# A fused attention and gated-FFN layer on one core: the ending of a sequence spread over three steps, and its TensorE pieces issued ahead of the value matmuls

## The chip, the core and the metric

The kernel runs on one core of a Trainium2 chip. A core has a matrix engine (TensorE, "PE" in the profile; its weight loads are "PEld"), a vector engine (VectorE, "DVE"), an engine for activations (ScalarE, "ACT"), a general engine (GpSimd, "POOL"), and a queue from which the transfers of this kernel are issued (SyncE, "SP"). Each engine takes its instructions in the order in which they were written, and waits at the head of its queue. The metric is the device time of one execution in microseconds (us).

## What is computed

The input x has 8 batches of 2048 tokens of 512 channels in fp32. Cut to what matters:

```python
xn = layernorm(x)
q, k = xn @ Wq.T + bq, xn @ Wk.T + bk          # 8 heads of 8 channels
v = xn @ Wv.T + bv                             # 8 heads of 64 channels
scores = leaky(q . k / sqrt(8), 0.2)           # per head, 2048 x 2048
s = gamma * (softmax(scores) @ v) + xn
ret = softmax(gate logits of xn), all but the largest of 4 set to 0
g = silu(xn @ W.T + sum_e ret[e] * (xn @ Wd[e].T) @ Wu[e].T)
out = x + s * g
```

## The kernel before, in words

**Sequences and steps.** A sequence `s` is one pair of heads on one block of 512 queries, so a batch has 4 pairs x 4 blocks = 16 sequences and the program 128. A sequence has 16 steps `i`, one for each 128 keys; the program has 2048 steps, all written out by one Python loop, with no scheduler behind it: `tc.manual_schedule()` keeps the written order on every engine. "Half step" in the change's title is one such step. In each step the loop issues, in this order:

- PE: subtract the row maximum from the scores of this step, first head (`less_max`, L658); scores of the next step (`score`, L641, two matmuls); one unit of row maxima of the next sequence (`max_unit`, L586, two matmuls, which VectorE reduces at L597 in 1.2 us); `less_max` for the second head.
- ACT: two exponentials of 512 columns (L670), then two leaky ReLUs of the next scores (L652).
- then one call of `half_full` (batches 0 to 6) or of `half_light` (the last batch, which has no next batch to project). It fills the rest of the step on PE: values, or pieces of other work.
- POOL: the exponentials are added up for the softmax's denominator (`add_up`, L702), in 15 of a sequence's 16 steps.

A **value** (`weigh`, L682) multiplies one step's exponentials with v; it runs some steps late, from the list `last`. One value is two matmuls, which the trace shows as four records.

**Pieces.** Three generators are advanced piece by piece: `queue[0]` is the *ending* of the sequence that has had its last value, `queue[1]` is `shift_rows` (row maxima made into a shift for the next sequence; L603 to L630), and `queue[2]` is the background work: `project_block` (q, k and v of the next batch) and `lift_block` (the gated FFN). What a generator yields is its state: IDLE (go on at any time), TINY or FREE or SLOW (a piece with a PSUM bank comes next), HOLD (in the middle of an accumulation), WAIT (vector work follows in the next step). A generator in HOLD or WAIT keeps the others out. `go_on` advances whoever is IDLE, and then one that is in WAIT, and says so by its result. `spent` and `due` keep the background work in step with a plan.

**One bank.** In the loop there is one PSUM bank for pieces, tag "m" (`ps_m`, one buffer). The ending's two tiles (`dps2`, `atp`) and every tile of the background work (`zps`, `pps`, `dps`, `nps`, `gps`, `rps`, `vps`, `tp`) go through it, so a piece's first matmul waits until the piece before has been read out for the last time. The row maxima have a bank of their own pair of banks (`mx`), one buffer too: the matmuls of one step wait for the L597 of the step before.

**The ending** (`ending`, L719 to L762). VectorE copies the sums of values out (L724); some idle turns later come two TINY pieces and a WAIT:

1. L737: four groups of small matmuls (8 records) sum the denominators over partitions; VectorE multiplies by a mask, adds up, and takes the reciprocal (L745, L747, L749).
2. L754: four transposes; VectorE multiplies by the reciprocal (L756) and adds xn (L757).
3. In the next step, after WAIT: VectorE multiplies by the gate (L760) and adds x (L761), and SP issues the store. L761 is the last reader of the bank.

In steps 1 and 2 `half_full` issues one value, then the piece (L861 to L864). In step 3 `go_on` returns true and `half_full` issues up to two values and nothing else. `half_light` goes on after `go_on` instead: in the same step it issues the next background piece, and one or two values.

`lift_block` yields WAIT as well: after the gate's softmax (L461), its pick (L472), and twice around the split of the expert outputs (L498, L504).

Of the kernel before, what the change touches and what calls it, by code (L numbers as in the profile page):

```python
# [12 lines left out]
ALU = mybir.AluOpType  # L13
# [19 lines left out]
def fused_layer_kernel(  # L33
# [37 lines left out]
    nc = tc.nc  # L71
# [3 lines left out]
    CH = NB * NT  # L75
# [168 lines left out]
    TINY, SLOW, WAIT, HOLD, FREE, IDLE = 5, 4, 3, 2, 1, 0  # L244
# [4 lines left out]
    def spend(cost):  # L249
        spent[0] += cost  # L250
# [273 lines left out]
    def where(s):  # L524
        return s // SEQ, s % NPAIR, (s % SEQ) // NPAIR
# [150 lines left out]
    def weigh(s, i, ex):  # L676

        if i == 0:
            avt[s] = ps_av.tile([128, BLK], FP, name="av")
        v_sb = vts[s]  # L680
        for e in range(2):
            nc.tensor.matmul(  # L682
                avt[s][64 * e : 64 * e + DV, :],
                lhsT=v_sb[:, i, 64 * e : 64 * e + DV],
                rhs=ex[:, e, :],
                start=(i == 0),
                stop=(i == CH - 1),
            )
        if i == CH - 1 and s + 1 < B * SEQ:
            assert queue[0] is None  # L690
            queue[0] = ending(s)
            state[0] = next(queue[0])
# [13 lines left out]
    def read_for_ending(s):  # L706

        b, p, n = where(s)
        if s >= B * SEQ or s in reads or (b, n) not in lifted:
            return  # L710
        cols = slice(p * 128, (p + 1) * 128)
        gs = two.tile([128, NT, 128], FP, name="gs")
        nc.sync.dma_start(out=gs, in_=GS[b][n][:, :, cols])
        xs = two.tile([128, 2, NT, 128], FP, name="xs")
        nc.sync.dma_start(out=xs[:, 0], in_=xv[b, n][:, :, cols])
        nc.sync.dma_start(out=xs[:, 1], in_=XN[b][n][:, :, cols])
        reads[s] = gs, xs

    def ending(s):  # L719

        b, p, n = where(s)
        cols = slice(p * 128, (p + 1) * 128)
        avs = two.tile([128, BLK], FP, name="avs")
        nc.vector.tensor_copy(avs, avt.pop(s))  # L724
        yield IDLE
        sums = acc.pop(s)
        while s not in reads:
            read_for_ending(s)
            yield IDLE
        gs, xs = reads.pop(s)  # L730
        for _ in range(3):
            yield IDLE
        yield TINY

        dps = ps_m.tile([128, 2, NT, 32], FP, name="dps2", tag="m")
        for q in range(4):
            nc.tensor.matmul(  # L737
                dps[32 * q : 32 * q + 32],
                lhsT=ones[:, 0:32],
                rhs=sums.rearrange("p e (t q j) -> p e t q j", t=NT, q=4)[:, :, :, q, :],  # L740
                start=True,
                stop=True,
            )
        dv = dps.rearrange("p e t j -> p (e t) j")
        nc.vector.tensor_tensor(dv, dv, diag.unsqueeze(1).to_broadcast([128, 2 * NT, 32]), ALU.mult)  # L745
        rd = sm.tile([128, NT, 2, 1], FP, name="rd")
        nc.vector.reduce_sum(rd.rearrange("p t e o -> p e t o"), dps, axis=AX.X)  # L747
        rd = rd.rearrange("p t e o -> p (t e) o")
        nc.vector.reciprocal(rd, rd)  # L749
        spend(0.5)  # L750
        yield TINY
        tp = ps_m.tile([128, NT, 128], FP, name="atp", tag="m")
        for t in range(NT):
            nc.tensor.transpose(tp[:, t, :], avs[:, t * 128 : (t + 1) * 128], ident)  # L754
        tv = tp.rearrange("p t (e d) -> p (t e) d", e=2)
        nc.vector.tensor_tensor(tv, tv, rd.to_broadcast([128, NT * 2, DV]), ALU.mult)  # L756
        nc.vector.tensor_tensor(tp, tp, xs[:, 1], ALU.add)  # L757
        spend(0.5)
        yield WAIT
        nc.vector.tensor_tensor(tp, tp, gs, ALU.mult)  # L760
        nc.vector.tensor_tensor(gs, tp, xs[:, 0], ALU.add)  # L761
        nc.sync.dma_start(out=ov[b, n][:, :, cols], in_=gs)  # L762

# [49 lines left out]
    def go(j):  # L813
        state[j] = next(queue[j], None)
        if state[j] is None:
            queue[j], state[j] = None, IDLE
        holder[:] = [k for k in range(3) if state[k] in (HOLD, WAIT)]

    def ahead():

        return holder or [k for k in (1, 0, 2) if queue[k] is not None and state[k] != IDLE]

    def go_on():

        for j in range(3):
            if queue[j] is not None and state[j] == IDLE:
                go(j)
        if holder and state[holder[0]] == WAIT:
            go(holder[0])
            return True  # L830
        return False
# [6 lines left out]
    last = []  # L838
    ended = [False]

    def values(count):
        for w in last[:count]:
            weigh(*w)
        del last[:count]

    def half_full():


        run = 0
        for w in last[:2]:  # L850
            run += 1
            if w[1] == CH - 1:
                break
        alone = run and last[0][1] == CH - 1
        if go_on():
            values(run)
            return
        j = (ahead() or [None])[0]
        if j == 2 and state[2] != HOLD and spent[0] > due[0] + AHEAD:
            j = None  # L860
        if j is not None and state[j] == TINY:  # L861
            values(min(run, 1))
            go(j)
            ended[0] = True  # L864
        elif j is None or len(last) > MUCH - (state[j] != HOLD) or (ended[0] and run > 1):
            ended[0] = False
            for g in stats.values():
                next(g, None)
            values(run)
        else:  # L870
            if alone:
                values(1)
            go(j)
            if state[j] == HOLD and not alone:
                go(j)
            ended[0] = state[j] != HOLD

    def half_light():

        begun = spent[0]  # L880
        go_on()
        late = last and (state[2] == SLOW or last[0][1] == CH - 1)
        if late:
            values(1)
        j = (ahead() or [None])[0]
        while j is not None and state[j] != WAIT and spent[0] < begun + 0.8 and (j < 2 or spent[0] < due[0]):
            go(j)
            if state[j] != HOLD:
                break
        if not late:  # L890
            values(2 if spent[0] - begun < 0.4 and len(last) > 1 and last[0][1] < CH - 1 else 1)
# [7 lines left out]
    with tc.manual_schedule():  # L899
# [143 lines left out]
        for s in range(B * SEQ):  # L1043
            for i in range(CH):
                if i <= 3 and s + 2 not in qst and (where(s + 2)[0] in (0, *ready) or i == 3):
                    load_stacks(s + 2)
                if i >= 6 and s + 1 not in vts and (where(s + 1)[0] in valued or i == 13):
                    load_values(s + 1)
                if i >= 12:
                    read_for_ending(s)  # L1050
                due[0] = due_at(s + (i + 1) / CH)
                u = s * CH + i + CH + LEAD
                nxt = s * CH + i + 1


                less_max(s, i, sc0, 0)
                if nxt < total:
                    sc1 = score(nxt // CH, nxt % CH)
                max_unit(u // CH, u % CH, flip=True)
                less_max(s, i, sc0, 1)  # L1060
                if u % CH == CH - 1 and u < total:
                    queue[1], state[1] = shift_rows(u // CH), IDLE
                ex = exp(sc0)
                if nxt < total:
                    leaky(sc1)
                if s < (B - 1) * SEQ:
                    half_full()
                else:
                    half_light()
                add_up(s, i, ex)  # L1070
                last.append((s, i, ex))
                sc0 = sc1
        values(len(last))
        for _ in ending(B * SEQ - 1):
            pass
# [44 lines left out]
```

## Time and profile before

| what | us |
|---|---|
| median of three runs (5580.12 to 5607.04) | 5593.03 |
| the profiled execution, its own time | 5602.28 |
| its span in the trace | 5600.5 |
| up to the first step of the loop | 139.5 |
| batches 0 to 6: 1792 steps | 4744.8 |
| last batch: 255 steps, up to the start of the last | 699.9 |
| the last step and the last ending | 16.3 |
| PE busy, POOL busy, ACT busy, DVE busy | 5408.1, 4778.7, 4440.4, 3678.3 |
| mean granted clock of PE | 0.961 |

The four stretches come from cutting the timeline at the first L658 matmul of each step. A row of a timeline reads: start, duration, engine, line, operation, tile written <- tiles read, shapes, count, and in brackets how long the engine had been idle before and whose end it was waiting for. A step is named below by what PE does in it after its fixed part, in records of the trace's lines: "one value", "two values", "two matmuls" of a projection.

### The profile page before, as it was taken

What the parts mean: (1) busy time and instruction counts of PE and PEld (TensorE: products, weight loads), DVE (VectorE), ACT (ScalarE), POOL (GpSimd) and SP (SyncE); (2) the same over time, 40 slices, a digit from 0 to 9 for tenths busy, and PEclk for the clock granted to TensorE, in tenths of its full rate; (3) what the DMA queues carried; (4) which work ended last, traced back from release to release, by engine and by line L of the source; (5) the groups of instructions that cost most, each with busy time, mean ns of one, the idle gap of its engine ahead of it and who ended that gap; (6) DMA issues with size and microseconds to landing.
All of it is one profiled execution on the core that took longest, in us unless ns stands there. A gap on an engine that the chain in (4) does not pass through costs nothing.

```text
span 5600.5 us, 78233 instructions
## 1 busy us (share of the span) xinstructions
PE 5408.1 (97%) x26258; PEld 2008.9 (36%) x26258; DVE 3678.3 (66%) x4990; ACT 4440.4 (79%) x8627; POOL 4778.7 (85%) x2906
## 2 busy tenths in 40 slices
PE   7999999999999999999999999999999999989998
PEld 3333333333333333333333333333333333333332
DVE  5577666667677666666666766676666766655653
ACT  1788888878888788887878878888788888867777
POOL 1789988888989888888988889898889898878878
PEclk9999999999999999998989989999999999989988
DMA  5333433434324343252422434225333333322221
GB/s 190 114 115 118 134 108 95 119 103 153 103 80 145 87 152 95 79 156 78 155 86 89 139 101 143 85 89 156 100 126 97 108 118 119 108 78 78 71 63 61
DMA packets 528265, 615.39 MB, mean 110 GB/s; under 512 B 44092, under 2 KB 438332, under 8 KB 491768
## 3 DMA queue, kind: packets, MB, share of 16 engines
q1 hardware_dynamic: 527864, 610.39, 35.3%
q8 instruction: 209, 3.42, 0.3%
q14 instruction: 192, 1.57, 0.1%
HBM read 407.88 MB, written 202.38 MB: 109 GB/s over the span
## 4 chain that ended last, share of the span: by engine, by line
PE 82%; ACT 7%; DVE 6%; issue 2%; DMA 1%; POOL 1%; SPq 0%; POOLq 0%; ACTq 0%; DVEq 0%
PE av L682 30%; PE sc L658 17%; PE zps L279 9%; PE vps L279 8%; PE mx L586 7%; ACT ex L670 4%; PE pps L265 2%; PE qkps L265 2%; PE dps L265 2%; ACT sc L652 2%; DVE mxr L597 2%; PE dps L737 1%; POOL acc L702 1%; PE atp L754 1%; PE gps L446 1%
## 5 line engine op out<-in xcount | busy, mean ns | idle before, releaser
L702 POOL TENSOR_TENSOR acc<-acc,ex 128x1024 f32<-128x1024 f32 x1792 | 4230.5, 2361 | 301.3 <-ACT ex L670 187.2
L597 DVE TENSOR_REDUCE mxr<-mx 128x2 f32<-128x1024 f32 x2030 | 2477.3, 1220 | 1249.9 <-PE sc L658 1017.6
L670 ACT ACTIVATE ex<-sc 128x512 f32<-128x512 f32 x4096 | 2229.2, 597 | 949.3 <-PE sc L658 772.0
L652 ACT ACTIVATE sc<-sc 128x512 f32<-128x512 f32 x4096 | 2238.0, 593 | 19.6 <-PE sc L641 19.6
L682 PE MATMUL av<-ex,v_sb 128*64 128x512 f32 x8192 | 2156.8, 632 | 11.6 <-DVE avs L724 9.2
L658 PE MATMUL sc<-shift,ones_r 2*128 2x512 f32 x4096 | 1683.7, 466 | 62.5 <-ACT sc L652 48.5
L586 PE MATMUL mx<-k,q_sb 32*128 32x512 f32 x4096 | 1460.6, 457 | 17.3 <-DVE mxr L597 11.9
L658 PEld LDWEIGHTS sc<-shift,ones_r 2*128 2x128 f32 x4096 | 706.2, 188 | 1555.7 <-ACT sc L652 1455.0
L641 PE MATMUL sc<-q_sb,k 32*128 32x512 f32 x4096 | 1046.7, 507 | 0.0
L682 PEld LDWEIGHTS av<-ex,v_sb 128*64 128x64 f32 x8192 | 469.8, 138 | 842.4 <-issue 807.9
L279 PE MATMUL zps<-w_sb,xnT 128*128 128x512 f32 (+1 forms) x1120 | 559.4, 614 | 23.8 <-DVE gs L761 10.5
L586 PEld LDWEIGHTS mx<-k,q_sb 32*128 32x128 f32 x4096 | 568.3, 189 | 38.8 <-DVE mxr L597 20.4
L702 POOL TENSOR_TENSOR acc<-ex 128x1024 f32<-128x1024 f32 x128 | 301.9, 2358 | 211.3 <-ACT ex L670 211.3
L279 PE MATMUL vps<-wv_sb,xnT 128*128 128x512 f32 x960 | 473.4, 617 | 7.4 <-DVE gs L761 7.2
L641 PEld LDWEIGHTS sc<-q_sb,k 32*128 32x128 f32 x4096 | 388.9, 187 | 0.8 <-issue 0.8
L279 PEld LDWEIGHTS zps<-w_sb,xnT 128*128 128x128 f32 x1120 | 192.2, 196 | 271.2 <-issue 250.6
L279 PEld LDWEIGHTS vps<-wv_sb,xnT 128*128 128x128 f32 x960 | 163.5, 189 | 207.7 <-issue 193.9
L518 DVE SCALAR_TENSOR_TENSOR g<-th,zps 128x512 f32<-128x512 f32 x128 | 88.0, 688 | 194.8 <-ACT th L517 194.8
L611 POOL TENSOR_TENSOR ml<-m,big 128x8 f32<-128x8 f32 x128 | 26.2, 205 | 133.5 <-DVE m L610 133.5
L265 PE MATMUL dps<-xnT,wd_sb 128*128 128x512 f32 (+1 forms) x280 | 138.6, 604 | 0.7 <-DVE gs L761 0.7
L349 DVE TENSOR_TENSOR vb<-vps,bv_sb 128x512 f32<-128x512 f32 x120 | 82.9, 691 | 85.5 <-PE vps L279 82.5
L265 PE MATMUL pps<-xnT,wp_sb 128*128 128x512 f32 (+1 forms) x280 | 130.9, 585 | 3.5 <-DVE gs L761 3.5
(124 smaller groups left out, 2675.8 us busy)
## 6 DMA issues: line engine op xcount, KB each, us to landing
v_sb<-VS SPq DMA_DIRECT2D x127, 1024.0 KB
k<-KS SPq DMA_DIRECT2D x256, 256.0 KB
XN<-xn SPq DMA_DIRECT2D x32, 1024.0 KB
q_sb<-QS SPq DMA_DIRECT2D x256, 128.0 KB
xnT<-XT SPq DMA_DIRECT2D x32, 1024.0 KB
GS<-g SPq DMA_DIRECT2D x32, 1024.0 KB
gs<-GS SPq DMA_DIRECT2D x128, 256.0 KB
xs<-in_x_dram SPq DMA_DIRECT2D x128, 256.0 KB
```

The lines of the kernel that those rows point to most:

```text
L265: nc.tensor.matmul(ps[:, part], lhsT=wt[:, c, :], rhs=xnT[c][:, part], start=(c == 0 and part.start == 0), stop=(c == NC - 1 and part.stop ...
L279: nc.tensor.matmul(ps[:, part], lhsT=xnT[c][:, t * 128 : (t + 1) * 128], rhs=wt[:, c, part], start=(c == 0 and part.start == 0), stop=(c = ...
L349: nc.vector.tensor_tensor(vb[:, :, t, :], ps.rearrange("p (h d) -> p h d", h=NPAIR), bv_sb.rearrange("p (h d) -> p h d", h=NPAIR), ALU.add,)
L518: nc.vector.scalar_tensor_tensor(g[:, t, :], th, 1.0, ps, ALU.add, ALU.mult)
L586: nc.tensor.matmul(parts[e], lhsT=q_sb[r, t * 128 : (t + 1) * 128], rhs=k_sb[r, kb // 2 * BLK : (kb // 2 + 1) * BLK], start=True, stop=True,)
L597: nc.vector.reduce_max(mxr[s][:, :, t, kb : kb + 1], mx, axis=AX.X)
L641: nc.tensor.matmul(sc[e], lhsT=k_sb[r, i // 2 * 128 : (i // 2 + 1) * 128], rhs=q_sb[r, :], start=True, stop=True,)
L652: nc.scalar.activation(sc[e], sc[e], AF.Prelu, alpha=SLOPE)
L658: nc.tensor.matmul(sc[e], lhsT=ones_r[r, :], rhs=shifts[s][r, :], start=False, stop=True, skip_group_check=True,)
L670: nc.scalar.activation(ex[:, e, :], sc[e], AF.Exp, scale=qscale)
L682: nc.tensor.matmul(avt[s][64 * e : 64 * e + DV, :], lhsT=v_sb[:, i, 64 * e : 64 * e + DV], rhs=ex[:, e, :], start=(i == 0), stop=(i == CH ...
L702: nc.gpsimd.tensor_tensor(acc[s], old, ex, ALU.add)
```

## The change

The ending's vector work is spread over one step more: the addition of xn moves from the transposes' step to the next, and the addition of x, with the store, from there to a third, behind a second WAIT. In `half_full` the ending's two TINY pieces are issued ahead of the value of their step (pieces of the background work still go behind it). In `half_light` a step in which `go_on` has resumed a generator from WAIT, of the ending or of the background work, issues values alone, two if two wait and the first isn't a sequence's last, else one, and returns.

```diff
@@ ending
         nc.vector.tensor_tensor(tv, tv, rd.to_broadcast([128, NT * 2, DV]), ALU.mult)
-        nc.vector.tensor_tensor(tp, tp, xs[:, 1], ALU.add)
         spend(0.5)
         yield WAIT
+        nc.vector.tensor_tensor(tp, tp, xs[:, 1], ALU.add)
         nc.vector.tensor_tensor(tp, tp, gs, ALU.mult)
+        yield WAIT
         nc.vector.tensor_tensor(gs, tp, xs[:, 0], ALU.add)
         nc.sync.dma_start(out=ov[b, n][:, :, cols], in_=gs)
@@ half_full
         if j is not None and state[j] == TINY:
+
+            if j == 0:
+                go(j)
             values(min(run, 1))
-            go(j)
+            if j != 0:
+                go(j)
             ended[0] = True
@@ half_light
         begun = spent[0]
-        go_on()
+        if go_on():
+            values(2 if len(last) > 1 and last[0][1] < CH - 1 else 1)
+            return
         late = last and (state[2] == SLOW or last[0][1] == CH - 1)
```

The built programs' order of instructions differs as follows. In batches 0 to 6, 111 endings of each kernel have both pieces in this loop; the counts of steps by content are nearly the same before and after (two values 618 and 616, one value alone 105 and 119, ending pieces 222 and 222), but the order of them around endings and gates isn't. In the last batch the steps with one value alone go from 66 to 81, and those with two or three matmuls of `zps` beside a value from 18 to 35.

## The prediction

> **What bounds the kernel.** I read the page first: its shares, and the slices of the granted clock.
>
> ```profile
> span 5600.5 us, 78233 instructions
> ...
> PE 5408.1 (97%) x26258; PEld 2008.9 (36%) x26258; DVE 3678.3 (66%) x4990; ACT 4440.4 (79%) x8627; POOL 4778.7 (85%) x2906
> ...
> PEclk9999999999999999998989989999999999989988
> ```
>
> PE is the bound on the whole, and its clock dips in some slices. Next I cut the timeline of all 2048 steps at their first L658. Undisturbed steps come out alike: two values 2.53 us, two projection matmuls 2.57, an ending piece with one value 2.24 to 2.47, one value alone 2.22 (ACT sets that one). Taking such a row for each step of batches 0 to 6 gives 4444 us; they took 4745. The 300 between are the question. By place: 117 in 80 steps at half clock; at full clock 73 in the ending's three steps and the one behind (5, 22, 3 and 43); 110 elsewhere, most of it in runs of transposes, which the change leaves alone. The step behind the ending takes 3.10 us in the mean.
>
> Who waits for the ending's last vector instruction:
>
> ```profile
> L761 DVE TENSOR_TENSOR gs<-atp,xs x128: 690/691/693, 221.4 to 5596.1; 128x512 f32<-128x512 f32 x128
> ...
>   PEld gps L446: 13.0, 16
>   PEld vps L279: 12.5, 12
>   PE zps L279: 10.5, 9
> ...
>   PE nps L425: 8.2, 3
> ```
>
> Every one is a piece that needs the one bank. Then the worst case, in the timeline:
>
> ```profile
> 2564.43 2.16 DVE L609 TENSOR_SCALAR big<-m 128x8 f32<-128x8 f32 x1
> 2567.43 0.70 DVE L757 TENSOR_TENSOR atp<-atp,xs 128x512 f32<-128x512 f32 x1
> 2568.04 1.22 DVE L597 TENSOR_REDUCE mxr<-mx 128x2 f32<-128x1024 f32 x1
> 2569.31 0.76 PE L586 MATMUL mx<-k,q_sb 32*128 32x512 f32 x2 [1.70 <-DVE mxr L597]
> 2569.89 0.69 DVE L761 TENSOR_TENSOR gs<-atp,xs 128x512 f32<-128x512 f32 x1
> 2572.33 1.87 PE L446 MATMUL gps<-simn,pw 128*128 128x4 f32 x8
> ```
>
> A small instruction (L609) takes 2.16 us, its median being 0.16: it began inside a POOL addition (L702) and ended with it. VectorE is then too late for the step's maxima, and PE stands idle 1.70 us. What the clock does is in the stretches of this place (span, then PE, PEld, DVE, ACT, POOL busy, then granted clock):
>
> ```profile
> 2562.00:2565.50 3.50, 3.50 (x26) 1.70 (x24) 3.18 (x6) 2.89 (x7) 3.42 (x2) 1.00 0.00 0
> 2565.50:2569.40 3.90, 2.20 (x13) 0.57 (x9) 3.83 (x6) 2.32 (x5) 3.19 (x8) 1.00 0.00 0
> 2569.40:2600.00 30.60, 30.60 (x90) 10.85 (x90) 15.49 (x30) 16.58 (x33) 22.52 (x10) 0.50 0.22 62
> ```
>
> After 3.9 us with PE busy for 2.2, the clock is 0.50 for 30.6 us. Light steps stay under it: one value alone takes 3.06 instead of 2.22. The clock changes only at multiples of 3.41 us, and every such stretch with PE busy below 0.56 of it is followed by half clock, most of those above 0.8 are not.
>
> **The Trainium skill on this.** TensorE: Matmul & The Clock Gate (section "Why this matters for your kernels") asks for no PE-idle gap above some 3 us, one window of idleness being what halves the clock. By that a gap of 1.70 us could not have done it, the half clock would come from elsewhere and stay, and the sum below would be 5507. The row above contradicts it, so I go by the row.
>
> **Part 1, the ending over three steps.** Vector work per step before: L597 1.22 plus 0.43, 0.42, 0.20; 1.22 plus 0.70, 0.70; 1.22 plus 0.69, 0.69. The last two are 2.6 us each in steps of 2.47 and 2.53, so L761 ends 1.46 us into the fourth step, where a piece could start at 0.66. After: 1.92, 2.61, 1.91. The third sheds what the second left over: from a third step whose maxima are ready at 0.76, addition and L760 end 0.85 into the next, its L597 ends at 2.08 and the last addition at 2.77, which is 0.24 into the fifth. A piece there starts at 0.66 and finds the bank free. So the 43 us go, and the second and third steps' 3. SP's store moves by one step with its instruction; what stands behind it in that queue is the shift's small loads for a sequence that begins several steps later, cost nothing; if that cover were gone, one step, 2.5 us, an ending. The fourth step holds values alone: two in 82 of 111 endings, one in 29. That costs only if later steps get heavier; by the built order all counts together move the undisturbed sum by 0.7 us.
>
> **What follows from it, the half clock.** Of the 28 gates (`gps`) in batches 0 to 6, six stand directly behind an ending with the long L609 in its second step; their twelve steps take 35.2 to 43.4 us against 30.24 of an undisturbed row. A seventh (38.6) and four with three one-value steps around them lose another 22. In the built order after, no gate stands there: 13 follow the fourth step in the undisturbed row's own sequence, 8 stand behind matmuls as in rows that kept the clock, 7 have two steps of two values behind them. L609 stands three steps ahead of the ending in those six sequences. I keep four half-clock stretches of 3.3 us (as at the slow `nps` of step 819): 15 of 117.
>
> **Part 2, the ending's pieces ahead of the value.** Undisturbed, nothing is won: in the last batch, where both orders occur, the two steps sum to 4.73 us either way (2.48 and 2.25, or 2.25 and 2.48). What is lost is cover: the first piece needs the bank, whose reader may not be done. After the last `zps` of a block L518 ends 1.43 into the step; after `pps`, L421 at 1.58; after `dps`, L442 at 0.69. How long PE stands is shown in the last batch, where the piece went first already:
>
> ```profile
> 5136.82 0.75 DVE L421 TENSOR_SCALAR pw<-pps,bp_sb 128x512 f32<-128x512 f32 x1 [1.17 <-ACT pw L420]
> ...
> 5137.71 0.64 PE L737 MATMUL dps<-acc,ones 128*32 128x256 f32 x8 [0.98 <-POOL acc L702]
> ```
>
> PE starts about 0.11 behind L421; the additions it reads were done over 7 us before, so POOL, though named, isn't it. By the built order 21 endings follow such a `zps`, 7 a `pps`, 13 a `dps`: 21 x (1.54 - 0.66) + 7 x 1.03 + 13 x 0.14 = 27 us, 22 above what the first step lost. Where it stalls, ACT catches up and the second step is 0.2 shorter: 28 x 0.2 = 6 back. In 36 endings L609 and L610 (0.40 together) now stand ahead of the first piece's vector work, 0.15 each at the transposes: 5; in 14 of them POOL may still be behind from a norm (L310, 1.02), from 0 to 1.2 us each; I take 0.5, from the long L609s two steps behind a norm: 7. Of the other bound, a gain, nothing: the reciprocal comes earlier, but its reader waits for L597.
>
> **Part 3, the last batch.** Its 255 steps took 699.9 us. There `half_light` starts the next piece in the very step in which vector work is resumed, and PE meets its own wait: 17 steps of 4.77 to 7.40 us (gates, norms, splits, the first `zps` behind an ending), 62 over the 2.45 of their neighbours, and 18 steps at half clock behind them (ten of 3.06, eight of 4.21), 23 more. With values alone in such steps the wait lies under them. Given back: 17 more steps with a second or third `zps` matmul at 2.65 for 2.39, less 15 of one value at 2.22, so 2; new half-clock steps 5. That leaves 622. POOL then decides: 240 additions of 2.43 (five in 12.14) and 16 chains of six (1.7) and three norms give 614, just below.
>
> **Sum.** 139.5 ahead + batches 0 to 6: 4445 (undisturbed) + 110 + 27 + 16 (second step, 22 - 6) + 12 + 15 = 4625, + 622 + 16.3 = 5403; with the 1.8 between span and time, 5405, against 5602.3 of the profiled execution. That one lay 9 above the median; I leave it there, since the clock's luck is in both.
>
> **Rivals.**
> - *The half clock stays* (0.15). The stalls go, but light steps or the new stalls of Part 2 fall into as many of the 3.41 us stretches: 5405 + 102 = 5507. For it: the 28 new stalls of 0.9 to 1.0 leave PE busy for about 0.72 to 0.76 of a stretch, and such were followed by half clock about one time in six. Against it: dense steps follow, which at once restore the clock (3.3 us at step 819, not 13).
> - *POOL is the bound of the last batch* (0.10). Its chains wait for VectorE 1.05 us each (133.5 in 127 times), its norms 1.0: 614 + 17 + 3 = 634, so 5417. For it: 614 of 622. Against it: seven buffers of exponentials lie between.
> - *Slower: gates starve* (0.04). The fourth step eats the store of values, so gates run over one-value steps and every gate falls to half clock, as six did, at 11 us each: 28 x 11 = 308 instead of 15, giving 5698. It decides from about 19 gates on (197 / 11 = 18 beyond those kept); with 16 to 20 of them the time is within half a per cent, another 0.03. Against it: the built order has a step of two values behind every gate.
> - *The change doesn't do what it says* (0.06): a third step that VectorE enters late, so that the wait only moves to the fifth step. Then the 43 stay, and the half clock by half: 5405 + 43 + 51 = 5499.
>
> **Chances.** The forecast has 0.62. The range runs from 5350 (no half clock 15, no price for L609 12, the last batch at POOL's 614, and 20 of the 110 gone) to 5510, which takes in the first, second and fourth rival's times. Faster are the forecast and those three. Half a per cent, 28 us, is about what a measurement of this kernel can tell from no change. Faster 0.93, same 0.03, slower 0.04.
>
> **What would show it.** L761's successor no longer in the list of waits; the step behind the ending at 2.5; first pieces behind `zps` starting 1.5 into their step; PE's granted clock near 0.98; no step above 4.5 in the last batch. Wrong it is if the clock stays at 0.96, or if steps with one value follow gates in rows.

## The result, and the profile after

The change makes the kernel slower, by three quarters of a per cent. The median of six runs is 5635.03 us (5619.47 to 5662.39), against 5598.75 of six runs of the kernel before: a ratio of 1.0076, 95% interval 1.005 to 1.0101. The forecast was 5405, and its range ended at 5510. The profiled execution of the changed kernel took 5627.17, its span is 5625.2, and the mean granted clock rose only from 0.961 to 0.966.

The page of the kernel after: its span, the engines' busy time, the granted clock by slice.

```profile
span 5625.2 us, 78283 instructions
...
PE 5346.8 (95%) x26258; PEld 1977.6 (35%) x26258; DVE 3672.9 (65%) x4990; ACT 4447.3 (79%) x8627; POOL 4779.3 (85%) x2906
...
PEclk9999999999999999989999899999999999999999
```

PE does the same 26258 matmuls in 61 us less busy time, in a span that is 25 longer. So PE is idle 86 us more than before, and the time is to be looked for in waits. First, who waited for the ending's last vector instruction, now L762 (kernel after, instructions of that line):

```profile
L762 DVE TENSOR_TENSOR gs<-atp,xs x128: 647/680/691, 219.2 to 5620.8; 128x512 f32<-128x512 f32 x128
...
  PEld nps L425: 0.7, 3
  PEld gps L446: 0.7, 3
```

The long list that stood under L761 is gone, and the step behind the ending takes 2.47 us in the mean instead of 3.10. What the change was built to do, it does. Now rows from PE's list of waits in the kernel after (engine, its tile and line, whose end it waited for: us in all, times, longest):

```profile
PE mx L586 <- DMA q_sb<-QS: 63.2, 17, 7.3
PE tp L370 <- ACT xn L319: 47.0, 28, 1.7
PE dps L737 <- DVE g L518: 17.5, 21, 0.8
...
PE dps L737 <- DVE pw L421: 7.9, 8, 1.0
```

and the same pairs in the kernel before:

```profile
PE mx L586 <- DMA q_sb<-QS: 2.0, 2, 1.2
PE tp L370 <- ACT xn L319: 1.7, 1, 1.7
```

The lower two of the first list are the price that Part 2 had foreseen, each within 1 us: 21 waits of 0.83 and 8 of 1.0. The upper two are new, 106 us together, and nothing in the prediction names them. No line of the diff touches either.

**The norm.** One of the 28 waits at L370, all engines of the kernel after (start, duration, engine, line, and in brackets the idle time before and its end):

```profile
1145.68 1.08 PE L682 MATMUL av<-ex,v_sb 128*64 128x512 f32 x4
...
1147.55 1.53 ACT L319 ACTIVATE xn<-xt,nmr,rstd 128x512 f32<-128x512 f32 x2
...
1148.43 0.66 PE L370 MATMUL tp<-ident,xn 128*128 128x128 f32 x4 [1.67 <-ACT xn L319]
```

The first transposes of a projected block read what ACT's L319 has normalized. L319 is written at the end of a generator (`norm`), and `half_full` advances those generators only in its branch for values alone (`for g in stats.values(): next(g, None)`), not in a step that has resumed somebody from WAIT. One more WAIT an ending turns 111 steps of the first kind into steps of the second, while the work goes on at the same pace. The norm is then not finished when its block begins, `project_block` runs what is left of it on the spot, and L319 stands in the same step as the transposes that read it: in the built order so in all 28 blocks of batches 0 to 6, where before it stood 1 to 11 steps ahead in nearly all. What the wait costs is more than itself (kernel after, stretches: span, then PE, PEld, DVE, ACT, POOL busy, granted clock, DMA share, GB/s):

```profile
1143.00:1146.40 3.40, 3.40 (x16) 1.19 (x14) 2.51 (x3) 2.87 (x6) 3.24 (x2) 1.00 0.00 0
1146.40:1149.80 3.40, 1.73 (x14) 0.84 (x14) 1.27 (x3) 2.88 (x6) 2.34 (x1) 1.00 0.83 307
1149.80:1153.20 3.40, 3.40 (x14) 1.30 (x14) 1.89 (x3) 2.58 (x5) 2.35 (x1) 0.53 0.01 4
```

PE is busy for 1.73 of 3.40, and the next stretch runs at 0.53 of the clock.

**The loads of q.** The SP queue of the kernel after (SPq is an issue, its duration the time that the queue was held by it):

```profile
1090.89 1.30 SPq L338 DMA_DIRECT2D KS<-hi  x2
1092.30 1.20 SPq L338 DMA_DIRECT2D KS<-lo  x2
1093.54 0.57 SPq L343 DMA_DIRECT2D QS<-hi  x1
...
1095.38 0.84 SPq L343 DMA_DIRECT2D QS<-lo  x1
1096.27 0.52 SPq L389 DMA_DIRECT2D XN<-xn  x1
1096.83 0.70 SPq L390 DMA_DIRECT2D XT<-xnT  x1
1097.64 2.84 SPq L542 DMA_DIRECT2D k<-KS  x2
1100.53 2.98 SPq L548 DMA_DIRECT2D q_sb<-QS  x2
```

and PE beside it, a little later:

```profile
1103.31 0.50 PE L641 MATMUL sc<-q_sb,k 32*128 32x512 f32 x2
1110.69 0.79 PE L586 MATMUL mx<-k,q_sb 32*128 32x512 f32 x2 [6.89 <-DMA q_sb<-QS]
```

A block's split issues ten stores, the last two (XN and XT) of 1 MB each. Behind them stand the four loads of k and q that a later sequence needs. They are written at step 0 of a sequence, and the first row maxima that read them at step 5. Since the background work has moved against the sequences, the split's stores now start at step 0 or 14 in three of four blocks of a batch (0, 14, 14 and 7), and in those three nothing stands between them and the loads; before they started at steps 12, 6, 6 and 2 (in the first batch 14, 7, 7 and 3). The loads are issued 7 us late, their own issue takes 2.8 to 3.0 us for two where 1.3 is usual, and q lands 7 us behind it. All the long waits stand at step 5 of a sequence; in sequence 6 of every batch that step takes 10.8 to 11.9 us.

Cut into steps as for the prediction, with what it had forecast for each term, and with kernel e6, which is told below (us). The 12 us that the prediction put at the transposes are counted in the second step, where these stand. The undisturbed row is worked out from the counts of steps alone, so it can't show what went wrong.

| term | before | forecast | after | e6 |
|---|---|---|---|---|
| up to the loop | 139.5 | 139.5 | 138.1 | 138.1 |
| batches 0 to 6, undisturbed | 4444.2 | 4445 | 4444.9 | 4444.9 |
| half clock (steps) | 117.1 (80) | 15 | 198.9 (100) | 22.4 (12) |
| ending's first step | 4.9 | 27 | 47.4 | 35.9 |
| second, third step | 25.7 | 28 | 26.4 | 26.8 |
| step behind | 42.7 | 0 | 0.4 | 1.2 |
| elsewhere | 110.2 | 110 | 115.6 | 111.4 |
| last batch | 699.9 | 622 | 635.4 | 644.3 |
| last step and last ending | 16.3 | 16.3 | 18.0 | 16.1 |

The row of the half clock holds most of the wait for q (54 of 63 us), since the steps with the long waits end under it, and 10 of the norm's 47. The norm's other 37 stand in the row "elsewhere", which 39 of the 112 steps of transposes have left for the half clock. The row of the half clock is 184 above the forecast, and the whole is 222 above it. The time that the clock itself spent at one half rose less than the row: by the trace's clock records it was 262.4 us of batches 0 to 6 before and 308.7 after, 33.0 of these while PE waited for q. In e6 it is 42.5.

### The profile page after: what moved, and what is told of

The parts are those of the page before. It is cut to its first block, busy times and chain, and to the rows that moved or that the text cites. A ratio compares the mean times of both kernels' runs of the same rounds, so it can differ in the third digit from the quotient of the medians.

```text
span 5625.2 us, 78283 instructions
## 1 busy us (share of the span) xinstructions
PE 5346.8 (95%) x26258; PEld 1977.6 (35%) x26258; DVE 3672.9 (65%) x4990; ACT 4447.3 (79%) x8627; POOL 4779.3 (85%) x2906
## 4 chain that ended last, share of the span: by engine, by line
PE 83%; ACT 8%; DVE 3%; DMA 3%; issue 1%; SPq 1%; POOL 1%; ACTq 0%; POOLq 0%; DVEq 0%
PE av L682 30%; PE sc L658 17%; PE zps L279 9%; PE vps L279 8%; PE mx L586 7%; ACT ex L670 5%; ACT sc L652 3%; PE qkps L265 2%; PE pps L265 2%; DMA q_sb<-QS 2%; PE dps L265 2%; PE atp L754 1%; PE dps L737 1%; PE tp L370 1%; DVE mxr L597 1%
## 5 line engine op out<-in xcount | busy, mean ns | idle before, releaser
L702 POOL TENSOR_TENSOR acc<-acc,ex 128x1024 f32<-128x1024 f32 x1792 | 4231.5, 2361 | 270.8 <-ACT ex L670 154.9
L597 DVE TENSOR_REDUCE mxr<-mx 128x2 f32<-128x1024 f32 x2030 | 2484.3, 1224 | 1311.6 <-PE sc L658 1021.3
L658 PE MATMUL sc<-shift,ones_r 2*128 2x512 f32 x4096 | 1652.8, 463 | 77.8 <-ACT sc L652 67.1
L586 PE MATMUL mx<-k,q_sb 32*128 32x512 f32 x4096 | 1475.1, 453 | 67.1 <-DMA q_sb<-QS 63.2
L658 PEld LDWEIGHTS sc<-shift,ones_r 2*128 2x128 f32 x4096 | 694.2, 187 | 1668.9 <-ACT sc L652 1562.0
L586 PEld LDWEIGHTS mx<-k,q_sb 32*128 32x128 f32 x4096 | 579.7, 188 | 84.7 <-issue 71.2
L279 PE MATMUL zps<-w_sb,xnT 128*128 128x512 f32 (+1 forms) x1120 | 529.0, 589 | 7.9 <-DMA xnT<-XT 7.9
L702 POOL TENSOR_TENSOR acc<-ex 128x1024 f32<-128x1024 f32 x128 | 301.8, 2358 | 183.4 <-ACT ex L670 183.3
L518 DVE SCALAR_TENSOR_TENSOR g<-th,zps 128x512 f32<-128x512 f32 x128 | 88.0, 688 | 184.8 <-ACT th L517 184.8
L611 POOL TENSOR_TENSOR ml<-m,big 128x8 f32<-128x8 f32 x128 | 26.2, 205 | 208.9 <-DVE m L610 202.0
L373 DVE COPY xnT<-tp 128x512 f32<-128x512 f32 x112 | 77.3, 690 | 106.1 <-PE tp L370 105.7
```

Source lines behind the costliest of these rows:

```text
L279: nc.tensor.matmul(ps[:, part], lhsT=xnT[c][:, t * 128 : (t + 1) * 128], rhs=wt[:, c, part], start=(c == 0 and part.start == 0), stop=(c = ...
L518: nc.vector.scalar_tensor_tensor(g[:, t, :], th, 1.0, ps, ALU.add, ALU.mult)
L586: nc.tensor.matmul(parts[e], lhsT=q_sb[r, t * 128 : (t + 1) * 128], rhs=k_sb[r, kb // 2 * BLK : (kb // 2 + 1) * BLK], start=True, stop=True,)
L597: nc.vector.reduce_max(mxr[s][:, :, t, kb : kb + 1], mx, axis=AX.X)
L658: nc.tensor.matmul(sc[e], lhsT=ones_r[r, :], rhs=shifts[s][r, :], start=False, stop=True, skip_group_check=True,)
L702: nc.gpsimd.tensor_tensor(acc[s], old, ex, ALU.add)
```

## The experiments

Two theories stood against each other. *The order*: Part 1's extra step moves the background work against the sequences; the norm starves and the loads fall behind the stores, and both drag the clock down. *The pieces*: Part 2's stalls at the first pieces bring the half clock, as the first rival had it. Each ratio is against the kernel before on the same chip. The kernels are called e1 to e10.

**One part at a time.** The last batch's edit alone, on the kernel before (e1):

```diff
@@ half_light (kernel before)
-        go_on()
+        if go_on():
+            values(2 if len(last) > 1 and last[0][1] < CH - 1 else 1)
+            return
```

> The kernel before with the half_light edit alone (values alone in a step that resumed a generator); the ending keeps its two steps, and half_full its order. Theory: the change's gain is all in the last batch. Batches 0 to 6 stay at about 4745 us, the last batch's 255 steps go from 700 to about 640, so some 5540 us against 5600. Rival (the three-step ending is what frees the last batch): the wait for the bank only moves by one step and the last batch stays above 680, 5580 or more.

5529.70 against 5593.85, ratio 0.988 (0.9856 to 0.9904). The last batch went from 699.9 to 640.6 and batches 0 to 6 stayed (4744.8 and 4734.9). Part 3 does what was said of it.

The order of pieces and value alone, on the kernel before (e4):

```diff
@@ half_full (kernel before)
         if j is not None and state[j] == TINY:
+            if j == 0:
+                go(j)
             values(min(run, 1))
-            go(j)
+            if j != 0:
+                go(j)
```

> The kernel before with the half_full edit alone: the ending's two pieces go ahead of the step's value. The order of everything else is unchanged. Theory of the prediction: a stall of 0.9 to 1.0 us where a background piece's bank has not been read out (11 endings behind a zps, 25 behind a vps with 0.25, few others), less the 0.2 at the step behind: 5 to 20 us slower, 5605 to 5620. Rival (the half clock follows those stalls): 50 or more slower. Rival (earlier denominators shorten the ending's chain on VectorE): 20 or more faster.

5574.42 (nine runs) against 5593.85, ratio 0.9958 (0.9939 to 0.9978): 20 faster, where the theory and the first rival had it slower; the second rival had the size. The first step rose from 4.9 to 32.2, 18 of it behind a `zps` or a `vps`, which had been priced at some 17. But with both vector steps of the old ending beginning earlier, the second step fell from 22.3 to 10.7 and the step behind from 42.7 to 22.0; with the third step's 7.9 more the four cancel. The rest is half clock, 117 to 65 in the profiled execution, which lies 20 below its own median; how much of that is luck stays open. The gates were not all spared (timeline of this kernel; L610 is held by POOL's addition to its end at 2547.97, and the maxima come 1.52 late):

```profile
2543.16 4.81 POOL L702 TENSOR_TENSOR acc<-acc,ex 128x1024 f32<-128x1024 f32 x2
2545.49 0.16 DVE L609 TENSOR_SCALAR big<-m 128x8 f32<-128x8 f32 x1
2545.69 2.32 DVE L610 TENSOR_SCALAR m<-m 128x8 f32<-128x8 f32 x1
...
2550.52 0.50 PE L586 MATMUL mx<-k,q_sb 32*128 32x512 f32 x2 [1.52 <-DVE mxr L597]
```

What follows: on the ending of two steps Part 2 isn't a loss, so the theory of the pieces falls here; e6 below shows the same for the ending of three.

The three-step ending alone, on the kernel before (e5):

```diff
@@ ending (kernel before)
-        nc.vector.tensor_tensor(tp, tp, xs[:, 1], ALU.add)
         spend(0.5)
         yield WAIT
+        nc.vector.tensor_tensor(tp, tp, xs[:, 1], ALU.add)
         nc.vector.tensor_tensor(tp, tp, gs, ALU.mult)
+        yield WAIT
         nc.vector.tensor_tensor(gs, tp, xs[:, 0], ALU.add)
```

> The kernel before with the ending's edit alone (three half steps); half_full's and half_light's orders as before. Theory: this part alone shifts the background work against the sequences, so that the norm and the loads of q and k come late in batches 0 to 6, as in the changed kernel; the last batch stays near 700. Some 60 to 100 us slower than before: 5655 to 5695. Rival (the lateness comes from the three parts together): within 20 of before, about 5595. The prediction's view of this part alone (the fourth step's stall goes): 40 to 100 faster.

5652.96 against 5595.59, ratio 1.01 (1.0084 to 1.0116). PE's waits in this kernel:

```profile
PE mx L586 <- DMA q_sb<-QS: 59.4, 18, 8.5
PE tp L370 <- ACT xn L319: 47.0, 28, 1.7
```

Both waits come with this edit: in e1 and e4 the first is 1.8 and 3.2, the second 1.7. The other direction, the changed kernel with the two-step ending of before (e10):

```diff
@@ ending (changed kernel)
+        nc.vector.tensor_tensor(tp, tp, xs[:, 1], ALU.add)
         spend(0.5)
         yield WAIT
-        nc.vector.tensor_tensor(tp, tp, xs[:, 1], ALU.add)
         nc.vector.tensor_tensor(tp, tp, gs, ALU.mult)
-        yield WAIT
         nc.vector.tensor_tensor(gs, tp, xs[:, 0], ALU.add)
```

> The changed kernel with the ending's two half steps of before: pieces first and values alone stay. Theory (the three-step ending alone shifts the background work and makes the norms and the q loads late): batches 0 to 6 as in the kernel with pieces first alone, 4700 to 4730, the last batch 640 to 650: 5500 to 5540, and no wait for q or for the norm. Rival (each part spoils it): 5600 or more.

5504.41 against 5591.39, ratio 0.986 (0.9813 to 0.9908). The waits of this kernel:

```profile
PE mx L586 <- DMA q_sb<-QS: 4.7, 5, 1.5
...
PE tp L370 <- ACT xn L319: 1.7, 1, 1.7
```

Parts 2 and 3 together are worth 87, about the sum of e1 and e4 (64 and 19). Part 1 turns that into a loss of 36.

**One cause at a time, in the changed kernel.** The norm is fed in the steps that resume, too (e2):

```diff
@@ half_full (changed kernel)
         if go_on():
+            for g in stats.values():
+                next(g, None)
             values(run)
             return
```

> The changed kernel, with the norm generators of the next projection advanced also in half_full's steps that resume from WAIT, as they are in its value steps. Theory (two feeders starve since the steps after WAIT came in: the norm, and the q and k loads): the 28 first transposes of projection blocks no longer wait for the normalized rows, 28 x 1.75 = 49 us, and the half clock that follows such a stall goes too, some 60: about 5520 against 5635. Rival (the late q loads are the whole cause, at step 5 of a sequence): less than 25 us, 5610 or more.

5556.24 against 5593.85, ratio 0.9916 (0.9888 to 0.9943), 79 below the changed kernel. The wait of L370 for L319 has left the list; in the built order L319 now stands 11 to 19 steps ahead. The wait for q stays:

```profile
PE mx L586 <- DMA q_sb<-QS: 60.4, 19, 6.8
```

It fell short of the 5520 expected: in batches 0 to 6 83 went, 71 of it at half clock, but the last batch took 652.2 with 37 steps at half clock, where the changed kernel has 18. The order of the last batch is the same in both; among the kernels here that have it, from 13 to 37 of its steps were at half clock, and no run shows why.

The two big stores are issued at the end of the block (e3):

```diff
@@ project_block (changed kernel)
         split_keys(b, n, ps, hi, lo)
-        nc.sync.dma_start(out=XN[b][n], in_=xn)
-        nc.sync.dma_start(out=XT[b][n], in_=xnT)
...
         store_values(b, n, vb)
+        nc.sync.dma_start(out=XN[b][n], in_=xn)
+        nc.sync.dma_start(out=XT[b][n], in_=xnT)
```

> The changed kernel, with a projection block's two 1 MB stores (XN, XT) issued behind its values instead of right behind its q and k stores, so that the loads of q and k stand two transfers earlier in SP's queue and land beside 2 MB less. Theory: the 63 us that PE waits for q at step 5 of a sequence go, and some 40 of half clock behind them: about 5530 against 5635. Rival (the loads are late because the q and k stores themselves stand ahead of them): under 25 us, 5610 or more. Rival (the norm is the whole cause): no change.

5559.06 against 5593.85, ratio 0.9932 (0.9907 to 0.9957), 76 below the changed kernel, though short of the 5530 expected: batches 0 to 6 lost 70, 59 of it the wait. Its SP queue at the same place, and its waits:

```profile
1088.69 0.84 SPq L343 DMA_DIRECT2D QS<-lo  x1
1089.64 1.56 SPq L542 DMA_DIRECT2D k<-KS  x2
1091.25 1.26 SPq L548 DMA_DIRECT2D q_sb<-QS  x2
```

```profile
PE tp L370 <- ACT xn L319: 46.9, 28, 1.7
...
PE mx L586 <- DMA q_sb<-QS: 4.0, 4, 1.8
```

The loads of q are issued in 1.26 instead of 2.98, and their wait falls from 63.2 to 4.0. The eight smaller stores still stand ahead of them and hardly hurt: it is the 2 MB that do. Each edit takes its own wait away and leaves the other, so the two causes are separate, and both are shown.

Both edits together (e6):

> The changed kernel with both repairs: the norms advanced in the steps after WAIT too, and the two 1 MB stores behind the values. Theory (two causes, each with half clock behind it, which no single repair removed): batches 0 to 6 about 4600, the time 5395 to 5430, near the forecast of 5405. Rival (the causes only add): 79 and 76 off 5635, so 5480. Rival (they hide each other): 5530 or more.

5445.03 against 5595.59, ratio 0.9727 (0.9712 to 0.9741), 15 above the range expected. Of the two waits one of 1.0 us is left; the row of L518 is Part 2's:

```profile
PE dps L737 <- DVE g L518: 17.4, 21, 0.8
...
PE mx L586 <- DMA q_sb<-QS: 1.0, 1, 1.0
```

This is the kernel that the prediction had described: 40 above the forecast, and the table shows them, 18 in batches 0 to 6 and 22 in the last. The two repairs give 190 together and 155 one by one. The clock records say where the 35 more are: time at half clock in batches 0 to 6 falls from 308.7 by 133 in e2, by 68 in e3 and by 266 in e6, 65 more than the two singly. At the 117.1 lost in 262.4 of the kernel before, an estimate, that is 29 us. That both new stalls and the old ones share stretches at half clock would explain it; no run took that apart.

**Two more terms of the prediction.** The piece goes ahead only when the step before ended no piece, so that the bank is free (e7):

```diff
@@ half_full (e6)
-            if j == 0:
+            first = j == 0 and not ended[0]
+            if first:
                 go(j)
             values(min(run, 1))
-            if j != 0:
+            if not first:
                 go(j)
```

> The kernel with both repairs, and the ending's piece ahead of the value only where the step before ended no background piece (else behind it, as before the change; so the second piece goes behind its value too). Theory: the stall of 0.9 to 1.0 us at 28 endings goes, of the 32 to 49 us that the first step loses some 25: 5375 to 5400. Rival (the later second piece gives it back in the step behind): equal to the kernel with both repairs within 10.

5418.60 against 5595.59, ratio 0.9677 (0.9661 to 0.9693), 26 below e6, and 19 above the range expected. The first step fell from 35.9 to 4.5 and the second rose from 16.5 to 28.9, so the rival's giving back is there too, at 12 of 31. So Part 2 costs 19 by the steps and 26 by the medians here, where the third vector step has already freed the bank; in e4, where nothing else had, its price and its gain cancel.

The small instructions that POOL holds up leave VectorE (e8):

```diff
@@ shift_rows (kernel before)
-        nc.vector.tensor_scalar(big, m[:, :, 0], 0.0, SLOPE, ALU.min, ALU.mult)
-        nc.vector.tensor_scalar_max(m[:, :, 0], m[:, :, 0], 0.0)
-        nc.gpsimd.tensor_tensor(ml, m[:, :, 0], big, ALU.add)
+        nc.scalar.activation(ml, m[:, :, 0], AF.Prelu, alpha=SLOPE)
```

> The kernel before with the three instructions L609, L610 (VectorE) and L611 (GpSimd) put as one leaky ReLU on ScalarE, the same function of the row maximum. Theory: those two VectorE instructions are held up by a running GpSimd addition, 20 times by up to 2.2 us, and at six gates the half clock follows: 40 to 80 us faster, 5515 to 5555, and the steps of these six gates below 3. Rival (the gates fall to half clock by their one-value steps, whoever holds VectorE): under 20 faster.

5547.06 against 5595.59, ratio 0.9913 (0.9891 to 0.9935). In batches 0 to 6 half clock went from 117.1 (80 steps) to 41.9 (32), the rest stayed. All 28 steps with a gate took 2.65 to 2.91, where six had taken 4.87 to 7.06. The group of this line, first in the kernel before and then in this one (busy us, mean ns):

```profile
L609 DVE TENSOR_SCALAR big<-m 128x8 f32<-128x8 f32 x128 | 53.6, 418 | 0.0
```

```profile
L609 ACT ACTIVATE ml<-m 128x8 f32<-128x8 f32 x128 | 28.0, 219 | 24.6 <-DVE m L603 24.6
```

So the prediction's reading of the gates was right: the held-up L609 makes two thirds of the half clock of batches 0 to 6 (in the last batch its time stayed, 144 us before and 156 here). The edit takes L611 off POOL as well; the two weren't separated.

All of it, e7 with e8's edit (e9):

> The kernel with both repairs and the piece ahead only where the bank is free, with the shift's first three instructions on ScalarE as well. Theory: VectorE is no longer held up by GpSimd, but in this order the long L609s stood three steps ahead of the ending and cost little; what is won is GpSimd's 0.28 a sequence in the last batch and the rest of the half clock (27 in batches 0 to 6): 5385 to 5415, against 5419. Rival (the hold-ups still cost some 40, as in the kernel before): 5380 or less. Rival (ScalarE, which sets the one-value steps, pays for it): 5425 or more.

5404.01 against 5591.39, ratio 0.9663 (0.9634 to 0.9692), the fastest version here and faster than both kernels. The first line of its page, and PE's share:

```profile
span 5402.9 us, 78002 instructions
...
PE 5261.4 (97%) x26258; PEld 1961.5 (36%) x26258; DVE 3611.2 (67%) x4734; ACT 4454.6 (82%) x8755; POOL 4750.9 (88%) x2778
```

Its clock is 0.990, and 12 steps of batches 0 to 6 lose 22.1 us to half clock; 107.9 elsewhere, the runs of transposes most of all, are the largest thing left.

## Why the prediction was wrong, step by step

- **Part 1, the direct effect: right.** L761's waits (43 us) went, the step behind the ending is at 2.47 for a forecast of 2.5, and no long chain moved to the fifth step.
- **Part 1, "what stands behind it in that queue is the shift's small loads for a sequence that begins several steps later, cost nothing": this failed.** It followed the one store that the diff moves past the queue. But the extra step shifts every later piece against the sequences, and so which of SP's instructions stand ahead of which loads: ten stores came to stand ahead of k and q. 63.2 us of PE waiting instead of the 2.0 of before, 59.2 of which e3 takes away. The price named "if that cover were gone", 2.5 an ending, belongs to another mechanism.
- **The "other" 110 and the half clock's 15: the same omission.** I counted the steps by content and found the same sum within 0.7 (4444.9 by the table), and took from that that nothing else changes. The counts don't show that the norms are advanced in one branch only and that steps move out of it. 47.0 us of waits, which e2 takes away. With q's they brought new half clock: its row went up to 198.9 instead of down to 15, some 64 of it these waits themselves.
- **The half clock for the gates: right, hidden under the new one.** Before, 11 of the 28 gates had half clock in their own step or the next two; after, 3. In e6, where the new waits are gone, 22.4 of half clock stand against the 15 forecast, behind stretches in which PE was busy for 0.87 to 0.89, for a reason that no run shows.
- **Part 2: the price right, "nothing is won" only here.** The first step was put at 27. Behind a last `zps`, a `pps` and a `dps` it exceeds its row by 18.9, 7.4 and 2.2 in the kernel after, 28.5 in all. As a whole it has 35.9 in e6 and 47.4 after; 8.8 of the difference are waits for q, and 4 in e6 stand behind transposes, which had no price. The gap between the reader's end and PE's start is 0.14 in the prediction's own two rows, not 0.11. The 12 at the transposes came to 9.0 after (L754 waiting for L747) and 1.1 in e6. On the two-step ending it wins 12 and 21 in the steps behind, which I had not worked out since I priced it only behind Part 1.
- **Part 3: the mechanism right, the size off by 13.** Steps above 4.5 went from 17 to 1; the 17 summed to 59.8 above 2.45 each, not 62. The half clock of the last batch is the mis-sized term: 18 steps, 15.0 us in all above 2.45 each, for the 5 of new ones. Without it the batch takes 620.4; so it does in e6 (644.3 less 23.9) and 620.3 in e9 (632.0 less 11.7).
- **The rivals.** The first, half clock that stays through Part 2's stalls, had the right symptom and the wrong cause: e6 has all these stalls and 22 of half clock. The second, POOL as the bound of the last batch at 634, isn't seen: three kernels take 620 there once their half clock is taken off. The slower one, starving gates, did not occur; starving was right, but it was the norm that starved. No rival was a change of the order of issue on an engine or queue that the diff doesn't touch, so 0.93 for faster stood on checks of PE and VectorE alone.

**What the Trainium skill says, beside it.** TensorE: Matmul & The Clock Gate, section "What's actually happening", describes an activity window that runs freely, some 3.4 us long; the grid of 3.41 found here agrees. Its section "HAM oscillation — how this bites in real kernels" asks for no PE idle gap above some 3.4 us; here the rows decide against it: stalls of 1.67 us were enough in most cases, as counted below.

## What to carry to other kernels

Where a hand-written order gives work to "the steps that have nothing else to do", a change that takes such steps away starves whoever lives on them, though every step costs the same: list for each generator which branch advances it, and compare in the built order how far each producer stands ahead of its reader. Do the same for a shared queue: what stands ahead of each load, in bytes, and how many steps remain to its reader. A stall is to be priced with the clock behind it, and an edit that seems to lose should be tried with its side effects taken away before it is dropped: this one loses 36 as it stands and gains 151 with two lines moved and two added.

## What the runs showed of the hardware

- **A stall of 1.7 us costs more than itself.** 28 of them, 47.0 us, gave back 79 when e2 removed them. The clock is decided in stretches of 3.41 us on a fixed grid. In the kernel after, from the first step on and at full clock, 15 of 17 stretches with PE busy for 0.50 to 0.52 were followed by half clock, and of 73 between 0.69 and 0.85 none was (in the kernel before 4 of 55). The prediction's "every such stretch" below 0.56 was 12 of 12 in the kernel before, and is 26 of 29 in this one. PE's busy share isn't the whole rule: of 167 between 0.85 and 0.95, 9 were followed by it too, and in e6 all ten such drops come from there. Behind the stall shown at 1148 the clock was back after one stretch (first row); behind the 6.89 us at 1110 it stayed low in three, two of them with PE busy throughout. Why the second took longer wasn't tried (stretches of the kernel after, columns as above):

```profile
1153.20:1156.60 3.40, 3.40 (x20) 1.26 (x18) 3.00 (x4) 3.35 (x7) 2.12 (x1) 0.97 0.31 43
1109.30:1112.70 3.40, 2.01 (x7) 1.21 (x7) 1.18 (x2) 0.78 (x2) 0.00 (x0) 0.50 0.45 164
1112.70:1116.10 3.40, 3.40 (x14) 0.98 (x14) 1.01 (x5) 1.24 (x3) 2.60 (x7) 0.50 0.00 0
1116.10:1119.50 3.40, 3.40 (x12) 0.64 (x11) 2.45 (x3) 1.61 (x4) 3.27 (x2) 0.53 0.00 0
```

- **A small VectorE instruction can wait for a whole GpSimd one.** L609 and L610 (fp32 tensor by scalar, 128x8, 0.16 us) took up to 2.32 when begun inside an L702 of 2.36, and ended with it. In the kernel before, of 38 L609 begun inside one, 22 took over 0.3 us and ended with it; the other 16 began in its last 0.27 us. Of 90 begun with GpSimd idle, none was long. Reductions and reciprocals begun inside L702 kept their times (L597 1.22, L749 0.20). GPSIMD Engine Reference, section "Specifications", says that GpSimd's SBUF interfaces are shared with VectorE, with contention for VectorE instructions in a two-port mode or with two SBUF inputs. The holds fit that; whether L609 runs in such a mode no run here shows.
- **Issues stretch behind big stores.** The two loads of q took 2.98 us to issue behind 2 MB of stores and 1.26 without them, and landed some 7 us behind their issue.
